# A graph-attention kernel of two layers: the tail of the last batch rearranged, tiles shared with ScalarE and GpSimd, and closings moved

## The chip, the cores and the metric

One Trainium2 chip; the program runs on one of its cores. The metric is device time in microseconds (us) of one execution. TensorE multiplies matrices, VectorE (DVE), ScalarE (ACT) and GpSimd (POOL) do elementwise work, SyncE (SP) issues most of the DMAs. Each engine takes its own instructions strictly in program order; engines wait for each other by semaphores.

## What is computed

Eight batches of 2048 nodes with 256 features go through two layers. Layer 0 is attention in 4 heads of 64, with a softmax inside each chunk of 256 nodes (8 chunks), and layer 1 is graph attention with one softmax over the neighbours. Each layer ends in a residual and a norm. Shortened:

```
q, k, v = x @ WqT, x @ WkT, x @ WvT                        # per head
scores  = where(adj == 0, -10, clip(q . k / 8, -10, 10))   # chunks of 256 keys
ctx     = sum over chunks of softmax(scores) @ v
y       = layernorm(ctx @ WoT + x) * gamma + beta
x1      = layernorm(x + y)                                 # layer 0

Wh      = x1 @ W                                           # layer 1
e       = leaky_relu(s_src[i] + s_dst[j]);  e = -inf where adj == 0
h       = elu(softmax_j(e) @ Wh)
out     = layernorm(x1 + h)
```

## The kernel before

**Slots and pairs.** A batch's attention is 64 slots of one query group (512 nodes), one pair of heads and one chunk; two slots make a pair, so there are 32 pairs, p = 0 to 31. In a pair, `burst` lets TensorE make the scores of the next pair's four units into PSUM (L398), `evict` has VectorE clip and mask them (`pr`, L415), `exps` has ScalarE take the exponential (L438), `product` multiplies by the values (`pc`, L449), ScalarE copies the result (`raw`, L456), and `normalize` has VectorE take a reciprocal (`rd`, L466) and GpSimd scale and add it up (`part`, `acc`, L473 and L475). All PSUM tiles of two banks come in turn from three pairs of banks (`two_banks`).

**Layer 1** of batch b runs beside the attention of batch b+1. Class `Layer1` has 8 units (two halves of the nodes times 4 heads) of 16 tiles, 128 tiles in all. `make` builds a tile `e` of 128 x 1024: VectorE takes the larger of a row (`srow`, a row of DRAM broadcast to all partitions) and a per-partition factor `gd`, times the adjacency `et` (L855). `use` has TensorE multiply it by `waug` (L884, 32 matmul instructions a tile). A `step` makes and uses two tiles; `make` is two tiles ahead of `use`. When a unit ends, ScalarE copies its sums out of PSUM (L896), and `close`, a generator that advances by one `yield` a step, divides them (L909, L910), applies elu, and writes `h` (L928).

**The last batches.** For the last batch (b = 7), layer 1 of batch 6 runs along in pairs 0 to 22; 36 tiles (18 steps, `LATE`) are kept for the tail. Pairs 23 to 31 are attention alone. Then a list `order`, written out by hand, interleaves these 18 steps with what is left of layer 0: the older group of nodes, `before` (query group 2, pieces `early`: statistics, finish with a store of x1 to DRAM, a load of it in squares of 32, the transposition `x1T` by VectorE, values), and the last group, `group` (group 3, pieces `steps`: bias, output projection L600, add, norm `a`, scale by gamma, norm `b`, finish, transposition on TensorE, values L642), then `factors` (`fs`), which gives layer 1 of batch 7 its row in DRAM, `gd`, and the scaled `waug` (L737, L739 on GpSimd).

After it layer 1 of batch 7 runs alone (`alone`): 64 steps. There every third tile is made by ScalarE (two activations, L824 and L825) and GpSimd (product with `et`, L826), begun `LEAD` = 4 tiles ahead (`make_ahead`); for VectorE's tiles `lift` copies the row to PSUM first (`rowp`, L794). Tables give the step at which a closing (`Close`, four a batch: load of x1, addition L959, statistics L516 to L527, application and store) is done: `CLOSING_ALONE` has the four of batch 6, `ENDING` those of batch 7. The last two end in `last`, after the last tile.

Of the kernel before, what the change touches and what calls it, by code (L numbers as in the profile page):

```python
# [16 lines left out]
P = 128  # L17
# [4 lines left out]
def adj_resnorm_kernel(  # L22
# [55 lines left out]
    LEAD = 4  # L78
    n_banks = WIDE // QT
# [26 lines left out]
    turn_of, bank_of = [0], [0]  # L106

    def two_banks(shape, name):

        turn_of[0] = (turn_of[0] + 1) % 3  # L110
        return psA.tile(shape, F32, tag=f"psA{turn_of[0]}", name=name)
# [393 lines left out]
    class Norm:  # L505
# [6 lines left out]
        def stats(self, ks):  # L512
# [7 lines left out]
            if ks[-1] == QT - 1:  # L520
# [3 lines left out]
                nc.vector.tensor_scalar(self.rs, self.mv[:, :, 1], EPS, None, ALU.add)  # L524
                nc.vector.tensor_scalar(self.off, self.mv[:, :, 0], -1.0, None, ALU.mult)
# [222 lines left out]
    class Layer1:  # L748
        def __init__(self, b, gd, waug):
# [4 lines left out]
            self.alone = b == B - 1  # L754
# [19 lines left out]
        def start(self):  # L774
            self.load_row(0)
            if self.alone:
                self.lift(0)
                self.ngd = small.tile([P, H, NT], F32, tag="ngd", name="ngd", bufs=1)
                nc.vector.tensor_scalar(self.ngd, self.gd, -1.0, None, ALU.mult)
# [11 lines left out]
        def lift(self, n):  # L791
            if n < len(UNITS):
                self.lifted[n] = psA.tile([P, WIDE * P], F32, tag=f"psA{n % 2}", name="rowp")
# [16 lines left out]
        def by_pool(self, k):  # L810
            return self.alone and k % 3 == 2

        def make_ahead(self, k):

            while self.begun < min(k + LEAD + 1, TILES):
# [13 lines left out]
        def make(self):  # L829
# [9 lines left out]
            if not self.alone:  # L839
                self.load_edge(k + AHEAD_E)  # L840
                e = ep.tile([P, WIDE * P], F32, tag="e", name="e")
                row = self.rows[n]
            else:
# [60 lines left out]
        def close(self, u, raw):  # L904
# [4 lines left out]
            nc.vector.tensor_scalar(dn, raw[:, :, D:D1], 1e-30, None, ALU.max)  # L909
# [97 lines left out]
    class Closing:  # L1007


        def __init__(self, b, table):  # L1010
            self.b, self.table, self.of = b, table, {}

        def do(self, s, *kinds):
            for g, step, *more in self.table.get(s, ()):
# [10 lines left out]
                elif step == "stats":  # L1025
                    self.of[g].n.stats((0, 1, 2, 3))
# [17 lines left out]
    for g in range(NCH):  # L1044
# [37 lines left out]
    }  # L1082
    CLOSING_ALONE = {
        -1: [(g, "load", kT, g) for g in range(NCH)],
        1: [(0, "pool")],
        2: [(1, "pool")],
        3: [(0, "stats")],
        4: [(1, "stats")],
        5: [(0, "finish")],
        6: [(1, "finish")],  # L1090
        8: [(2, "pool")],
        9: [(3, "pool")],
        10: [(2, "stats")],
        11: [(3, "stats")],
        12: [(2, "finish")],
# [4 lines left out]
        37: [(0, "pool")],  # L1100
        38: [(1, "pool")],
        39: [(0, "stats")],
        40: [(1, "stats")],
# [236 lines left out]
```

## Time and profile before

Three runs gave 3708.56 us in the median (3708.34 to 3709.61). The profiled execution took 3715.49 us, with a span of 3713.7 us at a granted TensorE clock of 0.991.

| | us |
|---|---|
| profiled execution, span | 3715.5, 3713.7 |
| busy in the span: TensorE, VectorE, ScalarE, GpSimd | 3547.3, 3055.2, 2302.6, 1458.7 |
| 128x1024 tile of layer 1 on VectorE, row from SBUF (L855, median) | 1.277 |
| the same, row from PSUM | 1.273 |
| helped tile: two ScalarE activations, one GpSimd product (means) | 1.142 + 1.150, 2.146 |
| `pow` of 128x4 on GpSimd (L526, median) | 1.01 |
| product of `waug` on GpSimd (L739, median of 32; there are 4 a batch) | 1.92 |

A line of the timeline reads: start, duration, engine, line, operation, output<-inputs with partitions x elements, count, and in brackets how long the engine was idle before it and what released it. A line of waits reads: who waited, `<-`, for whom, then us in total, times, longest. A line of windows gives a stretch, its length, the busy time of each engine with its instructions, the granted clock, the DMA share and GB/s.

### The profile page before, as it was taken

How to read it: one execution, taken by the hardware profiler on the slowest of the kernel's cores; microseconds unless marked ns; L12 is line 12 of the kernel's file. 1: busy time of each engine (PE TensorE's matmuls, PEld its weight loads, DVE VectorE, ACT ScalarE, POOL GpSimd, SP SyncE). 2: the span in 40 equal slices, each digit the busy share in tenths (PEclk: the TensorE clock that was granted, in tenths of full speed). 3: DMA queues.
4: the chain of work that ended last, by engine and by line, in shares of the span. 5: the costliest groups of instructions: out<-in, count | busy, mean ns of one | idle time of the engine just before them, and what ended most of it. 6: DMA issues, size and time to landing. Idle time of an engine off the chain costs nothing.

```text
span 3713.7 us, 169348 instructions
## 1 busy us (share of the span) xinstructions
PE 3547.3 (96%) x76884; PEld 2630.8 (71%) x76884; DVE 3055.2 (82%) x3652; ACT 2302.6 (62%) x4119; POOL 1458.7 (39%) x1259
## 2 busy tenths in 40 slices
PE   8999999999999999999999999999999999998777
PEld 5666677776777677776777767777677776775677
DVE  5886689978889699896989969988689977896787
ACT  4786456655666566665666656666566665666376
POOL 0454233333333334333433423434333333334366
PEclk9999999999999999999999999999999999999998
DMA  7764344554545455554555545555455554543432
GB/s 184 169 138 84 107 142 140 149 120 144 155 137 147 99 170 151 151 145 104 163 150 143 141 121 167 145 147 126 130 149 145 148 131 138 150 143 95 142 119 90
DMA packets 692866, 512.33 MB, mean 138 GB/s; under 512 B 429616, under 2 KB 528304, under 8 KB 692144
## 3 DMA queue, kind: packets, MB, share of 16 engines
q1 hardware_dynamic: 642144, 467.80, 46.1%
q10 hardware_dynamic: 50000, 33.70, 2.9%
q8 instruction: 601, 9.85, 1.1%
q14 instruction: 121, 0.99, 0.1%
HBM read 440.27 MB, written 61.08 MB: 135 GB/s over the span
## 4 chain that ended last, share of the span: by engine, by line
PE 65%; DVE 15%; issue 4%; ACT 2%; DMA 1%; POOL 1%; DVEq 0%; ACTq 0%; SPq 0%; POOLq 0%
PE pa L884 19%; PE pc L449 18%; PE ps L398 16%; DVE pr L415 6%; DVE e L855 5%; PE pp L342 4%; PE pw L642 3%; PE po L600 3%; PE pv L358 2%; DMA et<-edgeD 1%; DVE h L928 1%; DVE qT L493 1%; DVE xg L588 0%; DVE y L620 0%; ACT raw L456 0%
## 5 line engine op out<-in xcount | busy, mean ns | idle before, releaser
L438 ACT ACTIVATE pr<-pr 128x1024 f32<-128x1024 f32 x960 | 994.8, 1054 | 449.7 <-DVE pr L415 381.8
L415 DVE SCALAR_TENSOR_TENSOR pr<-ps,slab 128x1024 f32<-128x1024 f32 x960 | 1116.5, 1204 | 127.8 <-PE ps L398 104.2
L855 DVE SCALAR_TENSOR_TENSOR e<-srow,gd,et 128x1024 f32<-128x1024 f32 x896 | 1175.4, 1344 | 22.7 <-PE pa L884 9.0
L884 PEld LDWEIGHTS pa<-waug,e 128*64 128x64 f32 x32768 | 1014.1, 140 | 240.3 <-issue 183.4
L884 PE MATMUL pa<-waug,e 128*64 128x65 f32 x32768 | 1067.5, 224 | 61.8 <-DVE e L855 42.9
L449 PE MATMUL pc<-vaug,pr 128*64 128x65 f32 x30720 | 994.6, 222 | 48.9 <-DVE pr L415 23.3
L449 PEld LDWEIGHTS pc<-vaug,pr 128*64 128x64 f32 x30720 | 944.6, 138 | 78.2 <-DVE pr L415 40.6
L398 PE MATMUL ps<-qT,kT 64*64 64x512 f32 x8192 | 951.7, 598 | 13.5 <-DVE pr L415 10.9
L473 POOL TENSOR_TENSOR part<-raw,rd 128x512 f32<-128x512 f32 x448 | 473.5, 1057 | 1232.3 <-DVE rd L466 1228.5
L398 PEld LDWEIGHTS ps<-qT,kT 64*64 64x64 f32 x8192 | 285.4, 132 | 501.0 <-issue 272.4
L456 ACT COPY raw<-pc 128x520 f32<-128x520 f32 x512 | 302.9, 592 | 537.3 <-PE pc L449 536.0
L475 POOL TENSOR_TENSOR acc<-acc,part 128x512 f32<-128x512 f32 x448 | 593.9, 1326 | 35.2
L466 DVE RECIPROCAL rd<-raw 128x8 f32<-128x8 f32 x512 | 99.6, 194 | 195.8 <-ACT raw L456 192.1
L473 POOL TENSOR_TENSOR acc<-raw,rd 128x512 f32<-128x512 f32 x64 | 66.8, 1044 | 362.0 <-DVE rd L466 362.0
L642 PE MATMUL pw<-w_sb,x1T 128*64 128x264 f32 (+1 forms) x800 | 125.1, 392 | 6.5 <-DVE x1T L300 5.0
L600 PE MATMUL po<-wo_sb,qT 128*64 128x256 f32 (+1 forms) x912 | 120.7, 381 | 1.6 <-DVE rd L466 0.8
L342 PE MATMUL pp<-xT,wk_sb 128*128 128x512 f32 x256 | 118.8, 608 | 2.5 <-DVE xT L312 1.3
L342 PE MATMUL pp<-xT,wq_sb 128*128 128x512 f32 x256 | 117.7, 603 | 0.0
L358 PE MATMUL pv<-wv_sb,xT 128*128 128x256 f32 x512 | 117.4, 382 | 0.0
L920 ACT ACTIVATE sums<-sums,dn 128x64 f32<-128x64 f32 x448 | 117.1, 334 | 0.4 <-ACT y L564 0.4
L826 POOL TENSOR_TENSOR e<-e,et 128x1024 f32<-128x1024 f32 x42 | 90.0, 2146 | 48.4 <-ACT e L825 39.6
L642 PEld LDWEIGHTS pw<-w_sb,x1T 128*64 128x64 f32 (+1 forms) x800 | 83.7, 153 | 33.8 <-issue 5.3
(140 smaller groups left out, 2567.5 us busy)
## 6 DMA issues: line engine op xcount, KB each, us to landing
et<-edgeD SPq DMA_DIRECT2D x896, 256.0 KB, 3.5
slab<-clipD SPq DMA_DIRECT2D x256, 256.0 KB, 4.3
srow<-rowD SPq DMA_DIRECT2D x64, 512.0 KB, 5.1
xg<-in_x_dram SPq DMA_DIRECT2D x32, 512.0 KB, 5.5
x1D<-y ACTq DMA_DIRECT2D x32, 512.0 KB, 3.0
ctxD<-acc ACTq DMA_DIRECT2D x56, 256.0 KB, 3.9
ctx<-ctxD SPq DMA_DIRECT2D x224, 64.0 KB, 4.0
xp<-in_x_dram SPq DMA_DIRECT2D x224, 64.0 KB, 2.5
```

The costliest lines, as they stand in the source:

```text
L342: nc.tensor.matmul(pps[c], lhsT=w[:, kc, c * P : (c + 1) * P], rhs=st["xT"][:, kc, :], start=(kc == 0), stop=(kc == KC - 1),)
L398: nc.tensor.matmul(ps[z * D : (z + 1) * D, k, :], lhsT=kT[rows, hp, t * P + z * D : t * P + (z + 1) * D], rhs=qT[rows, hp, cols], start=Tr ...
L415: nc.vector.scalar_tensor_tensor(pr, ps, -CLIP, row.unsqueeze(1).to_broadcast([P, 2, CH]), op0=ALU.max, op1=ALU.min,)
L438: nc.scalar.activation(pr, pr, AF.Exp, scale=0.125)
L449: nc.tensor.matmul(pc[z * D : (z + 1) * D, k, to], lhsT=probs[s][u][:, k, i * P + z * D : i * P + (z + 1) * D], rhs=vaug[:, KT * c + u, 2 ...
L456: nc.scalar.copy(raws[s].rearrange("p k i d -> p k (i d)"), pc[:, :, : QT * D1])
L473: nc.gpsimd.tensor_mul(part, raw[:, :, :, :D], rd.to_broadcast([P, 2, QT, D]))
L475: nc.gpsimd.tensor_add(accv, accv, part)
L600: nc.tensor.matmul(po[z, k, :], lhsT=qT[:, c, t * P + z.start : t * P + z.stop], rhs=wo_sb[:, c, :], start=(c == 0), stop=(c == KC - 1),)
L642: nc.tensor.matmul(pw[z, k, : F + 2 * H], lhsT=self.x1T[:, c, u * P + z.start : u * P + z.stop], rhs=w1_sb[:, c, :], start=(c == 0), stop= ...
L855: nc.vector.scalar_tensor_tensor(e, row, self.gd[:, h, j : j + 1], self.mask(k), op0=ALU.max, op1=ALU.mult,)
L884: nc.tensor.matmul(self.pa[i // QT][z * D : (z + 1) * D, i % QT, :], lhsT=e[:, i * P + z * D : i * P + (z + 1) * D], rhs=self.waug[:, j, h ...
```

## The change

There are four parts. **Late tiles**: a method `go_late` is called as the second piece of the tail. From the next whole unit on (tile 96) every third tile of batch 6 is made by ScalarE and GpSimd too, begun two tiles ahead, and the row of each unit is lifted to the third pair of banks, so that `two_banks` takes turns over two pairs only. VectorE's late tiles lie in the six buffers of `pr`, no longer in the three of `e`. **Order**: in the tail the pieces of the last group go ahead of those of the older group; the older group's scale and second addition move from the end of pair 31 into the tail; `factors` comes after 11 steps and not 13. **Small steps**: in the alone stage two small operations of each norm and the maximum of L909 go to GpSimd, the reciprocal comes a step later, and the negation of `gd` goes to ScalarE. **Closings**: groups 0 and 1 of batch 6 are closed in pairs 23 to 30 of the last batch by VectorE and ScalarE, no longer in the alone stage; the other closings get new steps.

```diff
     LEAD = 4
+    LEAD_LATE = 2
     n_banks = WIDE // QT
...
-    turn_of, bank_of = [0], [0]
+    turn_of, bank_of, pairs_of_banks = [0], [0], [3]
...
-        turn_of[0] = (turn_of[0] + 1) % 3
+        turn_of[0] = (turn_of[0] + 1) % pairs_of_banks[0]
         return psA.tile(shape, F32, tag=f"psA{turn_of[0]}", name=name)
...
-        def stats(self, ks):
+        def stats(self, ks, by_pool=False):
             sts = []
...
                 self.off = small.tile([P, QT], F32, tag="off", name="off_" + self.name)
-                nc.vector.tensor_scalar(self.rs, self.mv[:, :, 1], EPS, None, ALU.add)
-                nc.vector.tensor_scalar(self.off, self.mv[:, :, 0], -1.0, None, ALU.mult)
+                few = nc.gpsimd if by_pool else nc.vector
+                few.tensor_scalar(self.rs, self.mv[:, :, 1], EPS, None, ALU.add)
+                few.tensor_scalar(self.off, self.mv[:, :, 0], -1.0, None, ALU.mult)
                 nc.gpsimd.tensor_tensor(self.rs, self.rs, nhalf, ALU.pow)
...
             self.tail = []
-            self.alone = b == B - 1
+            self.alone, self.late = b == B - 1, False
+            self.helped = 0 if self.alone else TILES
             self.halves = {}
...
                 self.lift(0)
-                self.ngd = small.tile([P, H, NT], F32, tag="ngd", name="ngd", bufs=1)
-                nc.vector.tensor_scalar(self.ngd, self.gd, -1.0, None, ALU.mult)
+                self.negate(small.tile([P, H, NT], F32, tag="ngd", name="ngd", bufs=1))
+
+        def negate(self, to):
+            self.ngd = to
+            nc.scalar.mul(to, self.gd, -1.0)
+
+        def go_late(self):
+
+            self.late = True
+            self.begun = self.made
+            self.negate(small.tile([P, H, NT], F32, tag="part", name="ngd", bufs=1))
+            n = self.made // NT + 1
+            self.helped = n * NT
+            self.lift(n)
...
             if n < len(UNITS):
-                self.lifted[n] = psA.tile([P, WIDE * P], F32, tag=f"psA{n % 2}", name="rowp")
+                k = n % 2 if self.alone else 2
+                self.lifted[n] = psA.tile([P, WIDE * P], F32, tag=f"psA{k}", name="rowp")
                 nc.scalar.copy(self.lifted[n], self.rows[n])
...
         def by_pool(self, k):
-            return self.alone and k % 3 == 2
+            return k >= self.helped and k % 3 == 2
...
-            while self.begun < min(k + LEAD + 1, TILES):
+            lead = LEAD if self.alone else LEAD_LATE
+            while self.begun < min(k + lead + 1, TILES):
                 t = self.begun
...
                 self.load_edge(k + AHEAD_E)
+            if not self.alone and not self.late:
                 e = ep.tile([P, WIDE * P], F32, tag="e", name="e")
                 row = self.rows[n]
+            elif self.late:
+                if j == 0 and n not in self.lifted:
+                    self.lift(n)
+                self.make_ahead(k)
+                if self.by_pool(k):
+                    return
+                e = prp.tile([P, WIDE * P], F32, tag="pr", name="e")
+                row = self.lifted.get(n, self.rows[n])
             else:
...
             dn = small.tile([P, n, 1], F32, tag="dn", name="dn")
-            nc.vector.tensor_scalar(dn, raw[:, :, D:D1], 1e-30, None, ALU.max)
+            (nc.gpsimd if self.alone else nc.vector).tensor_scalar(
+                dn, raw[:, :, D:D1], 1e-30, None, ALU.max
+            )
+            if self.alone:
+                yield 1
             nc.vector.reciprocal(dn, dn)
...
-        def __init__(self, b, table):
-            self.b, self.table, self.of = b, table, {}
+        def __init__(self, b, table, by_pool=True):
+            self.b, self.table, self.of, self.by_pool = b, table, {}, by_pool
...
                 elif step == "stats":
-                    self.of[g].n.stats((0, 1, 2, 3))
+                    self.of[g].n.stats((0, 1, 2, 3), self.by_pool)
                 elif step == "most":
...
     }
+    HOME_E = (ep, "e", 3)
+    CLOSING_PLAIN = {
+        23: [(0, "load", HOME_E)],
+        24: [(0, "add")],
+        25: [(0, "stats")],
+        26: [(0, "finish")],
+        27: [(1, "load", HOME_E)],
+        28: [(1, "add")],
+        29: [(1, "stats")],
+        30: [(1, "finish")],
+    }
     CLOSING_ALONE = {
-        -1: [(g, "load", kT, g) for g in range(NCH)],
-        1: [(0, "pool")],
-        2: [(1, "pool")],
-        3: [(0, "stats")],
-        4: [(1, "stats")],
-        5: [(0, "finish")],
-        6: [(1, "finish")],
-        8: [(2, "pool")],
-        9: [(3, "pool")],
-        10: [(2, "stats")],
-        11: [(3, "stats")],
-        12: [(2, "finish")],
+        -1: [(2, "load", kT, 0), (3, "load", kT, 1)],
+        6: [(2, "pool")],
+        8: [(3, "pool")],
+        9: [(2, "stats")],
+        11: [(3, "stats"), (2, "finish")],
         13: [(3, "finish")],
...
         30: [(g, "load", qT, g) for g in range(NCH)],
-        37: [(0, "pool")],
-        38: [(1, "pool")],
-        39: [(0, "stats")],
-        40: [(1, "stats")],
-        41: [(0, "finish")],
-        42: [(1, "finish")],
-        61: [(2, "most")],
-        62: [(3, "most")],
+        38: [(0, "pool")],
+        40: [(1, "pool")],
+        41: [(0, "stats")],
+        43: [(1, "stats"), (0, "finish")],
+        45: [(1, "finish")],
+        62: [(2, "most")],
+        63: [(3, "most")],
     }
...
         closing = Closing(b - 2, CLOSING) if b > 1 else None
+        plain = Closing(b - 1, CLOSING_PLAIN, False) if b + 1 == B else None
         if closing:
...
                 before, group = group, Between(b, q - 1, sd, waug)
-            if closing:
-                closing.do(p, "load")
+            for each in (closing, plain):
+                if each:
+                    each.do(p, "load")
             if i == 1 and q:
...
             hook(MIDDLE_OF, NEXT_MIDDLE)
-            if closing:
-                closing.do(p, "add", "factors")
+            for each in (closing, plain):
+                if each:
+                    each.do(p, "add", "factors", "stats")
             if i == 2 and q:
...
                     turns[0].pop(0)()
-                group.scale()
-                group.again()
+                    group.scale()
+                    group.again()
             product(s1)
...
             hook(FINALLY_OF, NEXT_FINALLY)
-            if closing:
-                closing.do(p, "sums", "squares", "finish")
+            for each in (closing, plain):
+                if each:
+                    each.do(p, "sums", "squares", "finish")
         normalize(SLOTS - 1)
...
             step = lower.step
-            order = [begin, early[0], lambda: coming.load_half(0, 0), step, ctx, early[1], step, steps[0], steps[1], early[2], step]
-            order += [steps[2], step, steps[3], early[3], step, steps[4], step, steps[5], early[4], step]
-            order += [steps[6], early[5], step, steps[7], early[6], step, steps[8], step, steps[9], step]
+            pairs_of_banks[0] = 2
+            order = [begin, lower.go_late, lambda: coming.load_half(0, 0), step, ctx, step, steps[0]]
+            order += [steps[1], before.scale, before.again, step, steps[2], lambda: group.a.stats(every)]
+            order += [steps[4], early[0], step, lambda: group.shift(), early[2], lambda: (group.scale(), group.again())]
+            order += [lambda: group.b2.stats(every), early[3], step, steps[6], early[4], step]
+            order += [early[5], steps[7], early[6], step, steps[8], step, steps[9], step]
             order += [fs[0], step, fs[1], step, fs[2], coming.start]
-            order += [step] * 5
+            order += [step] * 7
             assert sum(p is step for p in order) == LATE
```

## The prediction

> **What bounds the kernel now.** Read first the page's busy times, then busy time by stage, then inside each stage the waits and the work in order of time. TensorE is busy 96% of the span, but the change touches only the last 340 us, so the stages there decide:
>
> ```profile
> core 0: us, PE busy (x) PEld busy (x) DVE busy (x) ACT busy (x) POOL busy (x), PEclk, DMA share, GB/s
> 3456.60:3537.00 80.40, 58.05 (x1262) 50.68 (x1260) 68.83 (x89) 20.59 (x53) 24.43 (x15) 0.85 0.53 162
> 3537.00:3700.20 163.20, 132.66 (x4108) 130.01 (x4102) 134.31 (x170) 128.75 (x155) 122.14 (x69) 0.94 0.33 109
> ...
> 3370.20:3456.60 86.40, 73.77 (x1480) 48.09 (x1480) 49.19 (x65) 57.18 (x99) 40.51 (x37) 1.00 0.26 63
> ```
>
> 3370-3457 is pairs 23 to 31 of the last batch (attention alone), 3457-3537 the tail (36 tiles of batch 6 beside the last norms), 3537-3700 batch 7's 128 tiles alone. After that 13.5 us of ending are left as they are. In the tail VectorE is fullest (69 of 80 us) while ScalarE and GpSimd have 60 us free each. In the alone stage a tile takes 163.2/128 = 1.275 us, though 17 tiles in a row (544 matmuls) took 16.12 us, 0.95 each. What TensorE waits for there, and what VectorE waits for:
>
> ```profile
> PE pa L884 <- DVE e L855: 23.5, 10, 6.3
> ACT sums L896 <- PE pa L884: 17.8, 6, 10.9
> DVE dn L909 <- ACT sums L896: 15.8, 6, 3.9
> DVE st_c L516 <- POOL h L959: 9.2, 3, 5.6
> ```
>
> So VectorE stalls in order: on a unit's denominators (L909) and on a closing's addition (L959), and tiles queue behind. The longest of these, in order of time:
>
> ```profile
> 3550.08 1.40 DVE L516 BATCH_NORM_STATS2 st_c<-h 128x6 f32<-128x256 f32 x4 [5.63 <-POOL h L959]
> 3551.41 0.36 DVE L519 BATCH_NORM_AGGREGATE mv_c<-st_c 128x2 f32<-128x6 f32 x4
> ...
> 3552.15 2.83 DVE L928 SCALAR_TENSOR_TENSOR h<-ee,sums 128x512 f32<-128x512 f32 x1
> 3554.91 1.27 DVE L855 SCALAR_TENSOR_TENSOR e<-rowp,gd,et 128x1024 f32<-128x1024 f32 x1
> ```
>
> **Two rules of the skill.** "SBUF — State Buffer", Who interferes with whom: a VectorE instruction with two SBUF inputs, or in a two-port mode, and a GpSimd instruction that reads SBUF exclude each other for a whole instruction. The trace agrees: tiles from `srow` during GpSimd's `waug` products took 2.92 us each (5.84 for two, below), tiles from the PSUM copy `rowp` beside GpSimd's products 1.27 (mean of 86). I go by the trace: a late tile from PSUM costs 1.25 us whatever GpSimd does, but bias, scale, again and shift (two SBUF inputs) may each wait up to one GpSimd tile, 2.15 us. "TensorE: Matmul & The Clock Gate", What's actually happening: after about 3.4 us of idleness the array runs at half speed for as long. Here, after an idle 5.6 us, 64 matmuls took 3.74 us against 2.04 for 64 nearby; so a long gap costs some 2 us more than itself.
>
> **Two closings in pairs 23 to 30.** Added to VectorE: two additions (1.22, as L620) and two sets of statistics (four L516 1.40, four L519 0.36, two small 0.33: 2.1), together 6.6 us, all in the middle of a pair. Does it hide? A pair that has one 1.22 us step there:
>
> ```profile
> 3384.74 1.23 DVE L415 SCALAR_TENSOR_TENSOR pr<-ps,slab 128x1024 f32<-128x1024 f32 x1 [2.10 <-PE pc L449]
> 3385.88 1.22 DVE L617 TENSOR_TENSOR y<-y,gamma_sb 128x1024 f32<-128x1024 f32 x1
> 3387.02 1.22 DVE L415 SCALAR_TENSOR_TENSOR pr<-ps,slab 128x1024 f32<-128x1024 f32 x1
> ...
> 3388.28 2.81 PE L398 MATMUL ps<-qT,kT 64*64 64x512 f32 x24 [0.18 <-DVE pr L415]
> ```
>
> The second eviction frees the bank of the next burst. A pair without such a step takes 8.91 us from burst to burst (3370.22 to 3379.13), this one 9.15, and the next, whose reciprocal and first eviction were late too, 10.05 with a step of its own. So a step costs nearly its length: +6.6 (range 3 to 9). The loads are SP issues behind slab loads, DMA share 0.26: nothing. ScalarE's four applications (2.08) at pair 26 fit the 2.27 us it later waits for L415: nothing (2 if not). Those at pair 30 stand ahead of the copies of the last two products, where GpSimd's part, acc and the transposition L499 follow: +2.0. GpSimd's pow and product (1.0 + 0.2) lie in its 46 idle us: nothing.
>
> **The tail.** Where it waits:
>
> ```profile
> 3464.07 1.11 PE L499 MATMUL pt<-identf,acc 128*128 128x128 f32 x4 [5.56 <-POOL acc L475]
> ...
> 3477.69 4.88 SPq L282 DMA_DIRECT2D x1t<-x1D  x8
> ```
>
> ```profile
> 3492.00 1.25 DVE L300 STREAM_TRANSPOSE x1T<-x1t 128x1024 f32<-128x1024 f32 x1 [0.48 <-DMA et<-edgeD]
> ...
> 3493.30 3.69 PE L642 MATMUL pw<-w_sb,x1T 128*64 128x264 f32 x16 [5.03 <-DVE x1T L300]
> ...
> 3516.75 10.48 POOL L739 TENSOR_TENSOR waug<-waug,ed 128x1024 f32<-128x1024 f32 x4
> ...
> 3519.61 5.84 DVE L855 SCALAR_TENSOR_TENSOR e<-srow,gd,et 128x1024 f32<-128x1024 f32 x2
> ```
>
> Ten tiles leave VectorE: 10 x 1.27 = 12.7 us; so does L779 (1.89), while the late scale and again come in (2.4). But VectorE's sum is not what ends here. Followed on the clock of this trace: acc of the last slot ends 3464.0; ScalarE's negation (0.25, it reuses `part`) and lift (1.0) let tile 96 start at 3465.3. Then on VectorE two tiles 2.5, bias 1.2, scale and again 2.4, a tile 1.25, add 1.2, statistics 2.1: 3476; with 2 for locks against GpSimd tiles 3478. pow 1 to 2 and 0.3: 3480; ScalarE's apply 2.1, four unit scales 1.05, and only then the older group's finish 2.1: 3485 (now 3471.2, since that group went first). Its store lands in 3 to 5, eight loads issue in 4.9 and land in 3.0, the transposition takes 1.25: 3498, against 3493.25 now. VectorE waits in order at that transposition, and with it all its later tiles; TensorE has then used 12 tiles, not 14. From L642 to the row transposition TensorE is full: 22.8 us now with 12 tiles, 20.9 with 10. That point comes at 3519 (now 3516.1).
> After it 14 tiles are left instead of 10. Now they take 20.8 us, with 3.57, 1.70 and 1.53 us of waits since L739 locks the tiles out. In their place tile 119 is late: GpSimd makes it after copy and products of `waug` (1.0 + 4 x 1.92, the undisturbed median, + 2.15 = 10.9 us), while TensorE has five tiles, 4.7 us. So 13.3 + 6.2 + 1 of half clock = 20.5. Sum: the tail ends 2.5 us later, +4.5 with the 2.0 above. Bounds: -8, if the older group's trip through DRAM were hidden and only VectorE's saving counted; +12, if locks and queues delay each of the norms.
>
> **The alone stage.** Closings 0 and 1 are gone: the gap of 6.3 us before 3556.2 goes, and so does half clock behind it (8 tiles in 10.05 us instead of 7.6): -8.7. The other closings: `rs`, `off` cost VectorE 1.60 + 0.15, 1.36 + 0.16, 0.39 + 2.39 and 0.33 where they met GpSimd; together 6.4 us; a third slot between addition and statistics takes the remaining waits (0.62, 2.97). TensorE's gaps there are 2.7, 2.8 and 3.9; the statistics themselves (1.76 each) stay: -5. L909 on GpSimd, reciprocal a step later: TensorE's gaps behind L910 are 1.2, 1.0, 2.1, 2.4 and 0.6, 7.3 in all. The small operation on GpSimd isn't in the trace: 0.2 (product of 128x4, L527) to 1.0 (pow, L526), after a GpSimd tile of up to 2.15, with GpSimd's next tile and VectorE's reciprocal behind it; I take 0.2 and keep 2 of the 7.3: -5. Sum -19. Bounds: -25, the rate of 3590-3620 throughout (905/32 = 28 tiles in 30 us, 1.06 x 128 + 2.8 for the first GpSimd tile = 138.5); -9, closings 0 and 1 alone. Cover: ScalarE keeps 128.8 - 4.2 = 124.6 us of the new 144, 87%; in 3590-3620 it ran at 92%.
>
> **Sum.** +6.6 + 4.5 - 19 = -8 us. The profiled execution took 3715.5 (span 3713.7 and 1.8 around it), so 3707.5; it stands 6.9 above the median of the three runs, 3708.56, and the difference carries over: **3700.5**, 0.22% faster.
>
> **Rivals.** (1) The tail gains: TensorE's 26 us of idle time there are filled by the helped tiles, -8 instead of +4.5: 3688. For: 60 free us on ScalarE and GpSimd. Against: a transposition that waits for DRAM is ahead of VectorE's tiles. (2) The alone stage turns to ScalarE (129 of 163 us, in order, with waits on TensorE in it): only closings 0 and 1 pay, -9: 3710.5. Against: the 92% stretch. (3) Slower: in the tail the norms queue behind helped tiles. Four norms each need GpSimd's pow and ScalarE's application; with one GpSimd tile (2.15) and one ScalarE tile (2.3) ahead of each, 4 x 4.4 = 18 us more: 3718. It decides from about 4 us a norm, as gains elsewhere are 8. Against: ScalarE gets a pair of these instructions only every third tile. That the edit does nothing of what it says is excluded: order and engines are explicit.
>
> **How the numbers follow.** Mine 0.44 (3692 to 3708), rival 1 0.27 (3681 to 3692), rival 2 0.17 (3705 to 3716), rival 3 0.12 (3714 to 3726). A difference under 0.2%, 7.4 us, can't be told from none. Faster: 0.27 + two thirds of mine, 0.57; slower: 0.11 from rival 3 and 0.03 of the others, 0.14; same 0.29. The range 3684 to 3717 leaves out a fifth: the ends of rivals 1 and 3.
>
> **What would show it.** Pairs 24, 25, 28, 29 longer by 1.2, 2.1, 1.2, 2.1 us; `x1T` after `x1t` near 3507 on the new clock (pairs' 6.6 and 2.0 included), with VectorE idle before it; a late tile waiting for GpSimd behind L739; the alone stage near 144 us with no VectorE wait of over 2 us. Wrong if the tail is shorter than 78 us or longer than 92, or the alone stage over 152.

## The result, and the profile after

The changed kernel is slower: 3715.73 us in the median of 15 runs (3710.42 to 3722.0) against 3708.34 for the kernel before (15 runs, 3698.87 to 3711.97). The ratio is 1.0025, with a 95% interval of 1.0017 to 1.0033: +7.4 us, where -8 was forecast.

Its profiled execution took 3715.62 us with a span of 3713.8, the one before 3715.49 with 3713.7, so the two profiles seem equal. They aren't: the work ahead of pair 23, the same in both, ended 7.86 us earlier in this execution (pair 23's burst starts at 3362.36, before at 3370.22). So I compare lengths of stages, which repeat better. The pairs stage, with no edit in it, took 86.42 us in four profiles and 86.43 in a fifth, the old tail 79.7 to 80.9 (before, e3, e9, e10, e14; the last two with one more application in it), the alone stage all but unedited 162.9 to 163.5 (before, e2, e11). The changed stages repeat less well: the pairs with the closings on VectorE took 91.7 to 94.7 us in eight profiles, the changed tail 89.7 to 90.5 in four, the changed alone stage 154.0 to 156.3 in four (changed, e6, e7, e13). The same three stages after, by windows:

```profile
core 0: us, PE busy (x) PEld busy (x) DVE busy (x) ACT busy (x) POOL busy (x), PEclk, DMA share, GB/s
3362.40:3455.60 93.20, 75.64 (x1476) 48.36 (x1476) 54.46 (x85) 59.47 (x105) 42.74 (x40) 0.98 0.27 69
3455.60:3545.30 89.70, 58.18 (x1268) 51.05 (x1264) 54.70 (x79) 46.41 (x81) 40.99 (x25) 0.81 0.50 157
3545.30:3700.30 155.00, 130.12 (x4098) 126.18 (x4096) 119.58 (x134) 123.49 (x146) 118.66 (x78) 0.97 0.30 102
```

VectorE lost 14 us of work in the tail and 15 in the alone stage, as meant. Yet the tail, with TensorE doing the same, is 9 us longer. Read exactly (from pair 23's burst to the end of the last product, to the last late tile's release, to the last denominators):

| stage | before | forecast | after |
|---|---|---|---|
| pairs 23 to 31 | 86.42 | +6.6 | 93.35 (+6.9) |
| tail | 80.75 | +4.5 | 89.67 (+8.9) |
| alone | 162.87 | -19 | 155.02 (-7.9) |
| sum | 330.04 | -8 | 338.04 (+8.0) |

The waits of the alone stage after:

```profile
POOL e L843 <- ACT e L842: 29.6, 17, 7.1
DVE dn L940 <- POOL dn L935: 20.6, 7, 5.3
...
PE pa L910 <- DVE e L881: 11.5, 12, 1.8
...
PE pa L910 <- POOL e L843: 6.9, 5, 2.9
...
ACT qT L566 <- POOL off_c L529: 4.2, 1, 4.2
ACT kT L566 <- POOL off_c L529: 4.1, 2, 3.1
```

TensorE's wait for VectorE's tiles is halved (23.5 to 11.5 us), and the closing's statistics wait no longer (9.2 before). But VectorE still stands at the denominators, 20.6 us now and 15.8 before; the view names whoever came last, which is now GpSimd. New is ScalarE's wait for GpSimd's small steps, and TensorE's for helped tiles.

### The profile page after: what moved, and what is told of

Same layout as the page of the kernel before. It is cut to its first block, busy times and chain, and to the rows that moved or that the text cites. A ratio compares the mean times of both kernels' runs of the same rounds, so it can differ in the third digit from the quotient of the medians.

```text
span 3713.8 us, 169399 instructions
## 1 busy us (share of the span) xinstructions
PE 3544.0 (95%) x76884; PEld 2628.5 (71%) x76884; DVE 3032.7 (82%) x3628; ACT 2324.8 (63%) x4143; POOL 1474.2 (40%) x1282
## 4 chain that ended last, share of the span: by engine, by line
PE 64%; DVE 15%; issue 4%; ACT 3%; DMA 2%; POOL 1%; SPq 0%; DVEq 0%; ACTq 0%; POOLq 0%
PE pc L450 18%; PE pa L910 18%; PE ps L399 16%; DVE pr L416 6%; DVE e L881 5%; PE pp L343 4%; PE pw L644 3%; PE po L602 3%; PE pv L359 2%; DMA et<-edgeD 1%; DVE h L958 1%; DVE qT L494 1%; ACT e L841 1%; DVE y L622 0%; DVE xg L586 0%
## 5 line engine op out<-in xcount | busy, mean ns | idle before, releaser
L416 DVE SCALAR_TENSOR_TENSOR pr<-ps,slab 128x1024 f32<-128x1024 f32 x960 | 1117.0, 1205 | 128.8 <-PE ps L399 105.6
L881 DVE SCALAR_TENSOR_TENSOR e<-srow,gd,et 128x1024 f32<-128x1024 f32 x864 | 1133.6, 1344 | 11.8 <-DMA et<-edgeD 5.1
L881 DVE SCALAR_TENSOR_TENSOR e<-rowp,gd,et 128x1024 f32<-128x1024 f32 x108 | 131.6, 1271 | 22.4 <-DMA et<-edgeD 15.3
L843 POOL TENSOR_TENSOR e<-e,et 128x1024 f32<-128x1024 f32 x52 | 112.3, 2161 | 67.5 <-ACT e L842 44.8
```

What stands on the lines that cost most here:

```text
L416: nc.vector.scalar_tensor_tensor(pr, ps, -CLIP, row.unsqueeze(1).to_broadcast([P, 2, CH]), op0=ALU.max, op1=ALU.min,)
L881: nc.vector.scalar_tensor_tensor(e, row, self.gd[:, h, j : j + 1], self.mask(k), op0=ALU.max, op1=ALU.mult,)
```

## The experiments

"Before" and "changed" name the kernel that an edit starts from; ratios are to the kernel before, with 95% intervals. Units of the alone stage are counted from 0.

### Each part alone

**e1**: before, with closings 0 and 1 moved.

```diff
+    CLOSING_PLAIN = {23: [(0, "load", HOME_E)], 24: [(0, "add")], ... 30: [(1, "finish")]}
     CLOSING_ALONE = {
-        -1: [(g, "load", kT, g) for g in range(NCH)],
-        1: [(0, "pool")],
...
+        -1: [(2, "load", kT, 0), (3, "load", kT, 1)],
```

> The kernel before with closings 0 and 1 of batch 6 moved into pairs 23 to 30, all else as before. Stages before: pairs 23-31 86.4 us, tail 80.4, alone 163.2. Theory P (the prediction's terms): pairs +6.6, tail +2 (ScalarE's applications of pair 30 ahead of the last products' copies), alone -8.7: sum near 0. Theory W (the work is only moved: VectorE is as tight among the pairs as alone, and other waits fill the alone stage): pairs +6.6, alone -4 or less, sum +4 to +6.

Measured: ratio 1.0010 (1.0000 to 1.0019). Pairs 93.34 (+6.9), tail 82.76 (+2.0), alone 156.99 (-5.9), of which unit 0 gave 6.1 (27.2 to 21.1 us). Pairs and tail as forecast to 0.3 us; the gain is 5.9 and not 8.7, so moving the closings alone loses 3 us, between the two theories.

Where the gain in unit 0 fell short shows in TensorE's ninth to sixteenth tile there, before and in e1:

```profile
3556.23 10.19 PE L884 MATMUL pa<-waug,e 128*64 128x65 f32 x256 [6.33 <-DVE e L855]
```

```profile
3556.97 1.60 DVE L928 SCALAR_TENSOR_TENSOR h<-ee,sums 128x512 f32<-128x512 f32 x1 [5.55 <-ACT sums L926]
...
3559.82 7.69 PE L884 MATMUL pa<-waug,e 128*64 128x65 f32 x256 [1.47 <-DVE e L855]
```

The half clock behind the gap went as forecast: 10.19 us became 7.69. But the eight tiles start only 3.6 us earlier in the unit (15.3 us into it, 18.9 before), not 6.3. VectorE no longer waits for an addition; it waits 5.55 us at `h` for ScalarE's elu, and its next tiles stand behind that.

How the pairs pay is seen in the changed kernel's timeline, in pair 24:

```profile
3378.02 1.22 DVE L619 TENSOR_TENSOR y<-y,gamma_sb 128x1024 f32<-128x1024 f32 x1
3379.15 1.22 DVE L989 TENSOR_TENSOR h<-h,x1g 128x1024 f32<-128x1024 f32 x1
3380.29 1.22 DVE L416 SCALAR_TENSOR_TENSOR pr<-ps,slab 128x1024 f32<-128x1024 f32 x1
...
3381.56 2.81 PE L399 MATMUL ps<-qT,kT 64*64 64x512 f32 x24 [1.31 <-DVE pr L416]
```

The addition L989 stands ahead of the eviction L416 that frees the bank of TensorE's next burst; that wait was 0.18 in the like pair before, now 1.31. Pair by pair the sum hides misses: pairs 24, 25, 28 and 29 are longer by 1.1, 1.5, 0.3 and 3.7 us, where 1.2, 2.1, 1.2 and 2.1 were forecast. In pair 29 slower clock adds to the step. After the same wait the same matmuls took, in the changed kernel (granted clock 0.58) and in e4 (1.00), which run the same program there:

```profile
3436.52 3.29 PE L644 MATMUL pw<-w_sb,x1T 128*64 128x264 f32 x16 [2.03 <-DVE pr L416]
```

```profile
3439.86 2.00 PE L644 MATMUL pw<-w_sb,x1T 128*64 128x264 f32 x16 [2.03 <-DVE pr L416]
```

e4's pairs took 91.70 us. So the steps themselves cost some 5.3 us, and 1.6 of the 6.9 is clock behind their waits.

**e2**: before, with the tail's two parts (late tiles and order) alone.

```diff
-            order = [begin, early[0], lambda: coming.load_half(0, 0), step, ctx, early[1], step, ...
+            pairs_of_banks[0] = 2
+            order = [begin, lower.go_late, lambda: coming.load_half(0, 0), step, ctx, step, steps[0]]
...
```

> The kernel before with the tail alone changed (helped late tiles, new order, scale and second addition in the tail, two pairs of banks). Theory P: the tail 80.4 + 2.5 = 83 us, the rest as before. Theory Q (ScalarE's queue: lift(0) waits for the row's trip through DRAM with the activations of tile 119 behind it, and GpSimd's waug products ahead of its product): tail 86 to 88 us, of it over 24 between the row transposition and the last late tile (20.9 before), and the whole kernel 5 to 8 us slower.

Measured: 1.0016 (1.0008 to 1.0024). Tail 87.03 (+6.3; forecast for this part +2.5), pairs 86.42, alone 163.53. From the row's transposition to the last late tile it takes 25.5 us, so theory Q has the numbers; its mechanism is looked at below. The tail's rearrangement is a loss by itself; 6.3 and e1's 2.0 nearly give the 8.9.

**e3**: before, with the small steps on GpSimd, the reciprocal a step later and the new steps of `ENDING`.

```diff
-            nc.vector.tensor_scalar(dn, raw[:, :, D:D1], 1e-30, None, ALU.max)
+            (nc.gpsimd if self.alone else nc.vector).tensor_scalar(
+                dn, raw[:, :, D:D1], 1e-30, None, ALU.max
+            )
+            if self.alone:
+                yield 1
```

> The kernel before with the small steps alone changed: rs, off and the maximum of dn on GpSimd, the reciprocal a step later, the new steps of ENDING. Theory P: alone stage 163.2 - 10 = 153 us (or a little more, since closings 0 to 3 keep their steps). Theory Q (in order on GpSimd: dn stands behind helped tiles of 2.15 us each, so the reciprocal on VectorE waits as long as before, 20 us in the changed kernel against 15.8): alone stage 160 to 164 us.

Measured: 1.0002 (0.9993 to 1.0011), alone 162.71 (-0.2), as theory Q had it. A part that was to bring up to 10 us brings nothing. A wait in its alone stage:

```profile
DVE dn L915 <- POOL dn L910: 27.2, 7, 6.2
```

VectorE waits longer at the denominators than before (15.8). Each part alone comes to +3.0 (e1), +6.9 (e2) and -0.5 us (e3) over the three stages; together they gave +8.0.

### The tail

**e6**: changed, with no helped tile from 117 on.

```diff
-            return k >= self.helped and k % 3 == 2
+            return k >= self.helped and k % 3 == 2 and (self.alone or k < 117)
```

> The changed kernel without helped tiles from 117 on: 119, 122 and 125 go to VectorE, from the row in PSUM. Theory Q (these three tiles stand behind the products of waug on GpSimd and behind lift(0) on ScalarE, which waits for the row's trip): from the row transposition to the last late tile 25.2 us become 19 to 21, the tail 84 to 86. Theory D (the adjacency tiles et come late on SyncE's queue behind the row, whoever makes the tile): 24 to 26, the tail within 1.5 us of 89.7.

**e7**: changed, helped tiles kept, but the pieces in the old order.

```diff
-            order = [begin, lower.go_late, lambda: coming.load_half(0, 0), step, ctx, step, steps[0]]
+            order = [begin, lower.go_late, early[0], lambda: coming.load_half(0, 0), step, ctx, early[1], step, ...
```

> The changed kernel with the helped late tiles, but the pieces of the tail in the order of the kernel before (the older group first, its scale and second addition in pair 31, five steps at the end). Theory X (the older group's trip through DRAM, pushed behind the last group, costs): the transposition x1T 35 to 37 us after the stage's start and not 42, the row transposition 54 to 58 and not 64.5; tail 76 to 82 us. Theory Y (the help itself costs: lift, negation, locks and GpSimd's queue): x1T within 2 us of 42 or the tail still over 86.

**e11**: before, with the row lifted to PSUM in the tail, no help, old order.

```diff
+        def go_late(self):
+            self.late = True
+            self.lift(self.made // NT + 1)
```

> The kernel before with one thing of the change's tail: from tile 96 on VectorE takes the row from PSUM (lift, two pairs of banks for the rest, six buffers), but makes every tile itself, in the old order. Theory L (GpSimd's products of waug lock VectorE's tiles out while the row is in SBUF: waits of 3.57, 1.70, 1.53 us and half clock): from the row transposition to the last late tile 20.9 us become 14 to 16, the tail 80.75 becomes 74 to 77. Theory D (the adjacency tiles come late behind the row on SyncE's queue): 19 to 21, the tail within 2 us of 80.75.

**e13**: changed, with the adjacency of helped tiles in the slab buffers and one tile more of loads ahead.

```diff
-                et = edges.tile([P, WIDE * P], BF16, tag="et", name="et")
+                pool, tag = (slabs, "slab") if self.by_pool(k) else (edges, "et")
+                et = pool.tile([P, WIDE * P], BF16, tag=tag, name="et")
...
-                self.load_edge(k + AHEAD_E)
+                self.load_edge(k + AHEAD_E + self.late)
```

> The changed kernel, but in the tail the adjacency tiles of the helped tiles lie in the two slab buffers, which are free there, and not in the four edge buffers; every adjacency tile is loaded one tile earlier (four ahead, not three). Theory E (helped tiles hold the edge buffers: in the changed kernel SyncE's edge loads waited 12.4 us for GpSimd's products to free one, and VectorE's late tiles 12.1 us for their edges): the tail falls from 89.7 to 85 to 87 us, nearly all of it after the row's transposition (25.2 down to 21 to 23), and VectorE's waits for edges in the tail fall under 5 us; the time falls by as much against the changed kernel, ratio to the kernel before near 1.0015. Theory G (GpSimd's own queue: products of waug, then tile 119 and the tiles behind it): the waits for edges go, but the gap of TensorE of 7.6 us before tile 119 stays and the part after the transposition stays at 24 to 25 us, tail 89 to 90, ratio near 1.0025. Pairs 93.3 and the alone stage 155 in both.

Measured, in us; the row's transposition is counted from the start of the tail (in the changed kernel and e6, e7, e13 with the 2.0 of ScalarE's applications in it):

| | row's transposition | after it | tail | ratio (95%) |
|---|---|---|---|---|
| before | 59.5 | 21.3 | 80.75 | |
| e2 | 61.6 | 25.5 | 87.03 | 1.0016 (1.0008 to 1.0024) |
| changed | 64.4 | 25.3 | 89.67 | 1.0025 (1.0017 to 1.0033) |
| e6 | 65.5 | 22.1 | 87.58 | 1.0023 (1.0015 to 1.0031) |
| e7 | 61.8 | 22.3 | 84.09 | 1.0011 (1.0002 to 1.0020) |
| e11 | 58.3 | 20.8 | 79.11 | 0.9998 (0.9987 to 1.0008) |
| e13 | 63.1 | 25.8 | 88.88 | 1.0024 (1.0011 to 1.0037) |

The changed kernel's timeline of the tail, where it waits:

```profile
3497.82 1.25 DVE L301 STREAM_TRANSPOSE x1T<-x1t 128x1024 f32<-128x1024 f32 x1 [5.49 <-DMA x1t<-x1D]
...
3520.06 0.30 PE L735 MATMUL pr<-identf,sd 128*64 128x128 f32 x1
3520.34 2.34 PE L910 MATMUL pa<-waug,e 128*64 128x65 f32 x64
3523.80 3.02 PE L910 MATMUL pa<-waug,e 128*64 128x65 f32 x96 [1.12 <-POOL e L843]
...
3523.93 7.53 POOL L741 TENSOR_TENSOR waug<-waug,ed 128x1024 f32<-128x1024 f32 x4
...
3527.70 1.02 ACT L810 COPY rowp<-srow 128x1024 f32<-128x1024 f32 x1 [6.08 <-DMA srow<-rowD]
...
3530.93 1.15 ACT L842 ACTIVATE e<-e,gd 128x1024 f32<-128x1024 f32 x1
...
3532.21 2.13 POOL L843 TENSOR_TENSOR e<-e,et 128x1024 f32<-128x1024 f32 x1 [0.75 <-POOL waug L741]
...
3534.39 10.83 PE L910 MATMUL pa<-waug,e 128*64 128x65 f32 x283 [7.58 <-POOL e L843]
```

*Up to the row* the forecast holds: VectorE waits 5.49 us at `x1T` for the trip through DRAM. `x1T` comes at 3505.7 on the clock of before (3497.82 + 7.86; forecast 3507), the row at 3527.9 (forecast 3519 + 8.6). *After it* TensorE stands 7.58 us at tile 119, a helped tile, and two queues hold that tile up. GpSimd's `waug` products end at 3531.46. ScalarE's second activation for the tile ends at 3532.08, and GpSimd's product starts 0.13 us after that. ScalarE is late because it takes its instructions in order, and ahead of the activations stands `lift(0)`, the copy L810, which waits 6.08 us for the row of batch 7 to come back from DRAM. The view names `waug` for the 0.75 us, but by the clock ScalarE came last. e6 takes that tile from both engines: the part after falls by 3.2 us, and the gap by 4.0:

```profile
3538.23 13.98 PE L910 MATMUL pa<-waug,e 128*64 128x65 f32 x348 [3.57 <-DVE e L881]
```

What is left of the gap is VectorE, which had itself waited 4.58 us for that tile's adjacency. The tail fell by 2.1 us, between theories Q (84 to 86) and D.

e7 waits still longer for a helped tile, and its tail is 3.3 us over before's, between its two theories:

```profile
3513.38 7.53 POOL L741 TENSOR_TENSOR waug<-waug,ed 128x1024 f32<-128x1024 f32 x4
...
3520.04 1.02 ACT L810 COPY rowp<-srow 128x1024 f32<-128x1024 f32 x1 [7.56 <-DMA srow<-rowD]
...
3523.49 1.15 ACT L842 ACTIVATE e<-e,gd 128x1024 f32<-128x1024 f32 x1
...
3524.77 4.35 POOL L843 TENSOR_TENSOR e<-e,et 128x1024 f32<-128x1024 f32 x2 [3.87 <-issue]
...
3526.95 9.29 PE L910 MATMUL pa<-waug,e 128*64 128x65 f32 x256 [10.70 <-POOL e L843]
```

Here the `waug` products were done at 3520.91, and GpSimd stood idle for 3.87 us until ScalarE's activation ended at 3524.64. In all seven profiles with such a tile (changed, e2, e4, e5, e7, e8, e13) the product starts 0.13 or 0.14 us after ScalarE's activation and 0.75 to 3.9 us after the last `waug` product. So ScalarE's wait for the row set the gap (theory Q of e2), with GpSimd's products close ahead of it in the changed kernel: an estimate from this trace is that taking away either one alone would have gained at most 0.75 us.

With the 2.0 of the applications taken off, lift and help in the old order cost 1.3; the new order costs 5.6 more (89.67 against 84.09). e13 asked whether helped tiles hold the edge buffers too long: VectorE's waits for edges in the tail fell from 12.1 to 7.3 us, and nothing was gained after the row (25.8 us), since TensorE stands there as long:

```profile
3539.85 11.46 PE L912 MATMUL pa<-waug,e 128*64 128x65 f32 x290 [7.85 <-POOL e L845]
```

So the edge buffers were not it. The numbers are those of theory G, but they don't tell GpSimd's queue from ScalarE's; there too ScalarE's activation came last, 0.9 us after the `waug` products. No run here takes away ScalarE's wait alone.

e11 has no help, and its tiles from PSUM don't meet the lock. Yet the part after the row is only 0.5 us shorter than before, the numbers of theory D, though the adjacency was not the reason. Its waits in the tail:

```profile
PE pa L905 <- DVE e L876: 11.2, 4, 7.2
...
ACT rowp L805 <- DMA srow<-rowD: 7.3, 1, 7.3
...
DVE h L949 <- ACT sums L947: 6.5, 1, 6.5
```

ScalarE reaches the copy of batch 7's row and waits 7.3 us for it to come back from DRAM. The elu of a unit of batch 6 is behind that: its input was ready at 3506.7, and it started at 3515.20. `h` on VectorE is behind the elu, and late tiles behind `h`. The waits for the lock (3.57 + 1.70 + 1.53) gave way to one of 7.2 us. So the same trip of the row, through DRAM and ScalarE, stood ready to take the lock's place.

### The alone stage

**e4**: changed, maximum of the denominators back on VectorE, a step later, with the reciprocal. **e5**: e4, and the norms' two small steps back on VectorE too. **e8**: changed, but the four closings in the alone stage leave out the application of the norm, so that ScalarE has less work.

```diff
-            (nc.gpsimd if self.alone else nc.vector).tensor_scalar(
-                dn, raw[:, :, D:D1], 1e-30, None, ALU.max
-            )
             if self.alone:
                 yield 1
+            nc.vector.tensor_scalar(dn, raw[:, :, D:D1], 1e-30, None, ALU.max)
```

> The changed kernel with the maximum of dn back on VectorE, and both it and the reciprocal a step later than in the kernel before. Theory Q (the wait comes from GpSimd's queue): VectorE's waits at dn fall from 20.6 us to under 8, and the alone stage from 155.0 to 148-151 us. Theory R (VectorE's wait there is only slack, TensorE or ScalarE is the bound): waits fall, the alone stage stays within 2 us of 155.

```diff
-                    self.of[g].n.stats((0, 1, 2, 3), self.by_pool)
+                    self.of[g].n.stats((0, 1, 2, 3))
```

> The changed kernel with every small step back on VectorE (rs, off and the maximum of dn), the maximum and the reciprocal a step later than before. Theory G (the small steps stand in GpSimd's queue behind helped tiles and additions, so ScalarE's application waits for off, 4.2 us in unit 5, and the helped tiles behind it come late): unit 5 falls from 24.3 to about 22 us (22.2 in the kernel before), unit 1 by up to 1, the alone stage from 155.0 to 151-153. Theory V (VectorE is the bound, the prediction's): unit 5 and the stage get longer by 2 to 6 us.

```diff
-        def finish(self):
+        def finish(self, apart=False):
             o = self.x
-            self.n.apply(o)
+            if not apart:
+                self.n.apply(o)
```

> The changed kernel whose four closings in the alone stage leave out the application of the norm (16 activations, 8.3 us of ScalarE; the output of those rows is then x1 as loaded). Theory S (ScalarE and the helped tiles behind it bound the stage): the alone stage falls from 155.0 by 6 us or more, units 1 and 5 by 2 to 4 each. Theory V (VectorE bounds it): by less than 2.

Measured; unit 1 has closings 2 and 3 in it, unit 5 the first two of batch 7:

| | alone | unit 1 | unit 5 | ratio (95%) |
|---|---|---|---|---|
| before | 162.87 | 24.5 | 22.2 | |
| changed | 155.02 | 22.1 | 24.3 | 1.0025 (1.0017 to 1.0033) |
| e4 | 155.6 | 22.8 | 24.3 | 1.0029 (1.0017 to 1.0040) |
| e5 | 151.4 | 20.4 | 23.6 | 1.0017 (1.0007 to 1.0028) |
| e8 | 149.2 | 19.4 | 21.3 | 1.0016 (1.0009 to 1.0023) |

In e4 VectorE's wait at the denominators is halved, and the stage no shorter:

```profile
DVE dn L937 <- ACT sums L922: 10.3, 5, 3.3
```

So that stall was no longer what ended the units (theory R). e5 against e4 moves two operations a norm, 0.17 us each on VectorE, and gains 4.2. Its stage is where theory G put it, but unit 5 fell by 0.7 us and not by 2. e8 takes four applications, 8.3 us, from ScalarE and gains 5.8, in the units with closings, nearly as theory S had it. Both gains are larger than the 2.3 us by which the changed stage scatters. The path there runs through ScalarE and GpSimd. The changed kernel's timeline in unit 5:

```profile
3662.51 2.07 ACT L566 ACTIVATE qT<-h,off_c,rs_c 128x256 f32<-128x256 f32 x4
...
3666.88 4.35 POOL L843 TENSOR_TENSOR e<-e,et 128x1024 f32<-128x1024 f32 x2 [3.00 <-ACT e L842]
...
3668.93 0.63 ACT L922 COPY sums<-pa 128x260 f32<-128x260 f32 x2
...
3669.06 3.66 PE L910 MATMUL pa<-waug,e 128*64 128x65 f32 x64 [2.10 <-POOL e L843]
...
3671.31 0.25 POOL L935 TENSOR_SCALAR dn<-sums 128x8 f32<-128x8 f32 x1
3671.60 0.20 DVE L940 RECIPROCAL dn<-dn 128x8 f32<-128x8 f32 x1 [5.32 <-POOL dn L935]
```

ScalarE's application delays the next helped tile, GpSimd waits 3.00 us for it, TensorE 2.10 for GpSimd. The denominators (0.25 us) then stand behind GpSimd's second product, and VectorE behind them. Not all of VectorE's 5.32 us is GpSimd's doing: the unit's sums were out only at 3669.56. From there GpSimd's queue took 1.75 us and its operation 0.25; over seven units the maximum started 0.1 to 3.1 us after the sums, 12.1 in all. Nothing here is slow by itself: a small operation costs what is queued ahead of it.

### Versions built from the kernel before

**e9**: before, with the maximum and the reciprocal a step later, both on VectorE, and `ENDING`'s new steps. **e10**: e9, and closings 0 and 1 in the pairs by GpSimd (addition) and ScalarE (sums and squares, as other batches do it), the last application in the tail behind the last transposition of ctx. **e14**: e10, and the change's new steps for closings 2 and 3.

```diff
+            if self.alone:
+                yield 1
             nc.vector.tensor_scalar(dn, raw[:, :, D:D1], 1e-30, None, ALU.max)
```

> The kernel before with one thing of the change, and that on VectorE: in the alone stage the maximum and the reciprocal of dn come a step later (and ENDING has the new steps, a third slot between addition and statistics). Theory G (no small step in GpSimd's queue): alone stage 162.9 us minus 3 to 5, whole kernel 0.1% faster; units 1, 4 and 6 shorter by 1.5 to 2.5 each. Theory S (ScalarE and the helped tiles bound the stage wherever VectorE waits): within 2 us of 162.9.

```diff
+        24: [(0, "pool"), (0, "sums")],
+        25: [(0, "squares")],
+        26: [(0, "factors"), (0, "finish")],
...
+            order = [begin, early[0], lambda: coming.load_half(0, 0), step, ctx, lambda: plain.of[1].finish(), early[1], ...
```

> The same, and closings 0 and 1 of batch 6 moved into pairs 23 to 30 as in the change, but with the addition on GpSimd and the statistics on ScalarE, so that VectorE has only two small steps in a pair, and the last application in the tail. Theory M (what costs in the pairs is VectorE's 1.2 and 2.1 us between the two evictions, 6.9 in all): pairs 86.4 + 1 to 3 us, tail as before, alone stage 5 to 7 below the run without it. Theory A (ScalarE has no room in the pairs either): pairs 86.4 + 6 or more.

```diff
-        8: [(2, "pool")],
-        9: [(3, "pool")],
...
+        6: [(2, "pool")],
+        8: [(3, "pool")],
```

> e10 (small steps and denominators on VectorE, closings 0 and 1 in the pairs on GpSimd and ScalarE, old tail) with the change's new steps for closings 2 and 3 in the alone stage as well (6, 8, 9, 11, 13 in place of 8 to 13: a step more between each addition and its statistics). Theory S (the third slot was right by itself, and the loss came from GpSimd alone): the unit in which these closings fall takes 20.4 us, as in the run with all small steps back on VectorE (e5), and not 23.5 as in e10; the alone stage falls from 154.7 to 151 to 152 and the ratio to the kernel before from 0.9978 to near 0.997. Rival (the gain in e5 came from its reciprocal a step later or from the tail before it): the unit stays at 23 to 24, the alone stage at 154 to 155, ratio 0.9978. Pairs 87.0 and tail 81 in both.

| | pairs | tail | alone | unit 1 | ratio (95%) |
|---|---|---|---|---|---|
| e9 | 86.42 | 80.35 | 160.9 | 23.5 | 1.0001 (0.9989 to 1.0012) |
| e10 | 86.97 | 80.9 | 154.7 | 23.5 | 0.9978 (0.9971 to 0.9985) |
| e14 | 86.97 | 79.74 | 153.3 | 21.7 | 0.9972 (0.9965 to 0.9980) |

e9 gains 2.0 us in its stage, at the edge of its theory S, and its time can't be told from before's. Its stage is 1.8 us shorter than e3's, which has the small steps on GpSimd. e10 in the pair shown for e1:

```profile
3377.45 2.36 POOL L961 TENSOR_TENSOR h<-h,x1g 128x1024 f32<-128x1024 f32 x1
...
3382.07 2.81 PE L398 MATMUL ps<-qT,kT 64*64 64x512 f32 x24 [0.44 <-DVE pr L415]
```

On GpSimd the addition takes twice as long (2.36) and leaves TensorE a wait of 0.44 in place of 1.31: all of both closings costs the pairs 0.55 us, not 6.9 (less than theory M's 1 to 3), and the alone stage keeps its gain (6.2 below e9). e10 took 3697.74 us in the median against 3706.91, e14 3695.56 against 3705.97: 10.4 us less than before (a ratio whose interval overlaps e10's). Both kernels are faster than the changed one and the one before. In e14 unit 1, which repeats to 0.1 us (22.0 to 22.1 in the changed kernel, e6, e7 and e13), fell by 1.8 of the 3.1 us that theory S gave it: the new steps gain by themselves, but about half. Its shorter tail is no gain of the edit; there the same waits as in e10 were followed by less half clock.

## Why the prediction went wrong

- **Pairs, +6.6**: the sum right (+6.9), the mechanism in the main, the closeness in part luck: the steps cost some 5.3 us, spread otherwise over the pairs than forecast, and slower clock behind their waits, which the sum put at nothing, gave 1.6.
- **ScalarE's applications at pair 30, +2.0**: right (+2.0 in e1). The slack at pair 26 was right too.
- **Tail up to the row, +2.9 beside that 2.0**: right: +4.9 with it.
- **Tail after the row, "13.3 + 6.2 + 1 of half clock = 20.5"**: measured 25.3. Tile 119 behind `waug` was named; ScalarE's queue was not. There `lift(0)` waits 6.08 us for the row from DRAM with the tile's activations behind it, and these came later than the `waug` products. The tile was ready 14.3 us after the row, not 10.9: GpSimd first finished its own late tile 116 (3.7 us after the row), and waited 0.75 us for ScalarE at the end. The five tiles ahead of it took 6.75 us, not 4.7, with 1.12 of waiting for tile 116 among them; the wait was 7.58, not 6.2; the nine tiles behind it took 10.9, not 9.6, the half clock behind so long a gap costing 2.3 and not 1. That is 4.7 us, and the tail's whole error lies here: -0.3 forecast for this part, +4.0 measured (21.3 to 25.3).
- **Closings 0 and 1 out of the alone stage, -8.7**: measured -5.9. The half clock behind the gap brought its 2.4 (10.19 us became 7.69). Of the gap's 6.3 only 3.6 came back: behind the addition stood ScalarE's elu, and VectorE waits for that now.
- **Other closings and small steps, -5, and denominators on GpSimd, -5**: the step that failed most. Measured together -0.2 (e3), and -2.0 beside the moved closings (156.99 to 155.02). My sum charged GpSimd's small operation at its duration ("I take 0.2", measured 0.24) and kept 2 us for its queue. In the queue the maximum stood 1.5 to 3.1 us in six of seven units (12.1 in all), and ScalarE waits for `off` on the same queue. "After a GpSimd tile of up to 2.15" stood in the text as a bound, but nearly every unit pays it. With the same new steps and everything small on VectorE the stage takes 151.4 (e5): of the 10 us, 5.6 were there to be had beside the moved closings (e1's 156.99), and GpSimd gave 3.6 back. The other 4.4 didn't come even then; that ScalarE's work ends the units (e8 in the changed kernel) is the likely reason, but no run shows it beside e5's edit.

**The rivals.** Rival 2 came nearest in the alone stage: its -9 was -7.9, with ScalarE's stream of work a bound (e8). Its "against", the stretch at 92%, had no closing in it. Rival 3 gave nearly the right time (3718) by another mechanism: the norms didn't queue behind helped tiles, since `x1T` came when forecast; a helped tile at the end of the tail did, behind ScalarE's wait for the row and GpSimd's `waug`. Rival 1 is out. The text's own sign of error, an alone stage over 152 us, came true.

**The lock and the clock gate.** What the Trainium skill says in "SBUF — State Buffer", Who interferes with whom, is seen again in the tail: the older group's second addition (L622) took 3.04 us beside a GpSimd tile, the last group's 1.22. The rule was right and of little use: e11 gets out of its way in the late tiles and its time can't be told from before's. The other rule, on half clock behind a gap ("TensorE: Matmul & The Clock Gate", What's actually happening), held at the 7.58 us gap (2.3 us more, granted clock 0.77) and should have stood in the sum at that size. But waits shorter than its 3.4 us were followed by slow clock too: after the same wait of 2.78 us the same eight tiles took 7.69 us before (granted clock 1.00) and 8.91 in e1 (0.85). The measurement decides here.

## What to carry to other kernels

Work moved off a full engine costs what is queued ahead of it on the engine that takes it, not its duration: an operation of 0.24 us behind products of 2.15 us started up to 3.1 us after its input was there. Look at every engine that the moved work passes: tile 119 waited for GpSimd, as forecast, and a little longer for ScalarE, which stood at a copy for a DMA. Before moving work, look for an engine whose queue is idle at that very moment and whose delay nobody waits for; the same closings cost 6.9 us on VectorE between two evictions and 0.55 on GpSimd and ScalarE there.

When a wait is removed, look for the one that stands ready behind it; three times here it was ScalarE's (the elu in e1, the row in e11 and in the tail). And compare lengths of stages, but see first how well each repeats: here to between 0.01 and 3 us, where total times scatter by 10.

## What the runs showed of the hardware

- The work ahead of pair 23 ended between 3355.47 (e7) and 3370.22 us (before) in the profiled executions, where the program is the same up to there, while the unedited stage after it repeats to 0.01 us.
- After the same wait of 2.04 us, the same burst of 32 matmuls took 4.00 us in the changed kernel, e1, e4, e8 and e13, and 5.36 in e5, e6 and e7 (granted clock 1.00 in the changed kernel, 0.69 in e6), which accounts for the pairs stage of 93.3 in some and 94.6 in others; e4's 91.70 comes of the full clock in pair 29. Why the clock was granted differently isn't settled.
- A maximum or an addition of 128x4 to 128x8 mostly takes 0.22 to 0.25 us on GpSimd (0.56 and 0.61 in two) and 0.16 to 0.17 on VectorE alone; beside GpSimd's products single small operations on VectorE had taken up to 2.39 before.
